# A graph-convolution layer on one core: A kept in DRAM as 8 KB runs, row blocks woven in pairs, and sparse products in 64-row pieces, up to eight at a time

## The chip, the cores and the metric

The kernel runs on one core of a Trainium2 chip. The metric is the device time of one execution in microseconds, as the median of several runs; less is better. Before the change three runs gave 1476.8, 1478.03 and 1470.32 us, a median of 1476.8 us.

## The reference

The inputs are `x` (8 x 4096 x 256, f32), `adj` (4096 x 4096, f32) and `W` (256 x 256, f32). `adj` is sparse: an entry is there with a probability that falls with its row and with its column, on the diagonal always, so the first rows and columns hold far more entries than the last.

```python
HW = jnp.einsum('bnf,fo->bno', H, W)              # H is x
A_norm = jax.nn.relu((A + A.T) * 0.5)
D = jnp.sum(A_norm, axis=1)
d_inv_sqrt = jnp.where(D > 0, D_safe ** (-0.5), 0.0)
DAD = d_inv_sqrt[:, None] * A_norm * d_inv_sqrt[None, :]
L_norm = jnp.eye(N, dtype=H.dtype) - DAD
out = jnp.einsum('nm,bmo->bno', L_norm, HW)
x = _layernorm(x + jax.nn.relu(out), axis=-1)
```

So the last product multiplies a sparse 4096 x 4096 matrix with a dense one of 4096 rows and 8 x 256 = 2048 columns (one row is 8 KB).

## The kernel before, in words

**Dense stage.** `adj` is cut into 8 x 8 blocks of 512 x 512. For each pair of blocks (i, j), (j, i) with i <= j, SP's DMA queue loads both (line 506; 1 MB each, in runs of 2 KB), TensorE transposes one in 128 x 128 tiles into a PSUM bank (line 516), VectorE adds the other (line 520), ScalarE applies relu with the factor 1/2 (line 524), and VectorE sums each row over groups of 32 columns (line 527). The sums give the degrees and, as flags, which rows of A have anything in which group of 32 columns. ScalarE's queue stores the block to `a_dram`, a 4096 x 4096 matrix laid out by rows, in runs of 2 KB (line 533). Beside this runs `form(m)`, which loads 128 rows of x (line 609, two loads of 512 KB in runs of 1 KB), transposes them (line 616), multiplies by W (line 627), scales by the rows' factor, and stores 128 rows of the product to `g_dram` (runs of 8 KB). `multiply` adds up the first output block, block 0, densely while this goes on (line 585). VectorE also builds the lists of the first units here (from line 250 on).

**List stage.** Blocks 1 to 31 of 128 output rows are left. They are handled in 16 units, unit u of blocks 2u+1 and 2u+2 (the last of block 31 alone), in the order of the table `SEQ`. A block is four groups of 32 columns, so a unit has eight groups. For each unit there is a list of the rows of A that have an entry in some of its groups. A tile of the list is 128 rows, as two halves of 64; a half belongs to one kind, a set of groups out of 15 such sets (`KINDS`, with `CAPS` and `FIRST` for their room and place). For each tile GpSimd issues two indirect DMAs, the rows of A cut to the groups in question (`ga`, line 1032) and the full rows of the product (`g`, line 1047, 128 rows of 8 KB, 1 MB), into one of 12 slots of a ring. There are 256 tiles. The slots are given back in the order in which they were filled, and each gather waits for a product named by `gather_ahead`, so that gathers keep pace with the products.

`steps_of(u)` cuts the unit's products into steps. A step fills the array once: one product of 128 rows by 128 columns, two of 128 x 64, four of 128 x 32, or pieces of 64 rows. Each step runs over the four PSUM banks of 512 columns that a block's 2048 columns take, and an f32 product runs as two passes of the array (two records in the profile). Two blocks of rows, the 256 first rows, are kept in SBUF for all units (`g_hub`), and are multiplied whole as 128 x 128 (with `gh`, the rows of A for them). When a block's last product is done, `finish` has ScalarE evict four banks (line 788) and VectorE add the residual x, take the statistics and normalise (lines 798, 807, 831); SP's queue stores the result (line 841, 1 MB in runs of 1 KB), and the residual of a later block is loaded by ScalarE's queue (line 782, likewise). The lists of units that come five, four, three and two places later are built by VectorE and TensorE between the products (`classify`, `lists`, `prepare`, `collect`).

If a unit's lists find no room, a flag sends the program into a dense loop at its end, which this input doesn't reach.

What sets the order: each engine's instructions are put by hand behind the last one of its engine (`queue`), so the order of the code is the order on the engine. On ScalarE's queue stand the stores of A and of the products, then the loads of residuals between evictions; on SP's the loads of `adj` and x, then the stores of the output; on GpSimd's the gathers.

## Time and profile before

| what | value |
|---|---|
| median of three runs | 1476.8 us |
| span of the profiled execution | 1496.2 us |
| TensorE matmul busy (PE) | 1420.1 us, 95% |
| VectorE (DVE) | 1025.2 us, 69% |
| GpSimd (POOL) | 745.6 us, 50% |
| ScalarE (ACT) | 368.7 us, 25% |
| moved by DMA | 540.52 MB, mean 361 GB/s |
| of it by GpSimd's indirect queue q0 / SP's q1 / ScalarE's q10 | 281.94 / 126.62 / 130.58 MB |

The profiled execution has a span of 1496.2 us, 19.4 us above the median of the timed runs. The dense stage lasts until about 565 us; the first list product stands at 587 us, the last ends at about 1484 us, and the rest of the span is the last block's end. PE's busy time includes modelled ends of matmuls. A DMA share of 1.00 stands for 16 DMA engines busy with packets all the time; it can come out a few per cent above 1 in a short stretch. In the profile "issue" is time in which an engine waited for nothing that the profile shows.

### The profile page before, as it was taken

How to read it: one execution, taken by the hardware profiler on the slowest of the kernel's cores; microseconds unless marked ns; L12 is line 12 of the kernel's file. 1: busy time of each engine (PE TensorE's matmuls, PEld its weight loads, DVE VectorE, ACT ScalarE, POOL GpSimd, SP SyncE). 2: the span in 40 equal slices, each digit the busy share in tenths (PEclk: the TensorE clock that was granted, in tenths of full speed). 3: DMA queues.
4: the chain of work that ended last, by engine and by line, in shares of the span. 5: the costliest groups of instructions: out<-in, count | busy, mean ns of one | idle time of the engine just before them, and what ended most of it. 6: DMA issues, size and time to landing. Idle time of an engine off the chain costs nothing.

```text
span 1496.2 us, 20479 instructions
## 1 busy us (share of the span) xinstructions
PE 1420.1 (95%) x6768; PEld 757.9 (51%) x6768; DVE 1025.2 (69%) x3010; ACT 368.7 (25%) x462; POOL 745.6 (50%) x1547
## 2 busy tenths in 40 slices
PE   7998988979999999999999999999999999998996
PEld 6777877766777764333333334333333333333342
DVE  4767558889596752356569678789898079797454
ACT  4555545434544460010100100100110011001102
POOL 2444010010322336756577677577677646666762
PEclk9999999989999999999999999999999999999998
DMA  9999999999999999979899899999999979988995
GB/s 340 360 377 381 406 346 337 393 385 338 379 356 341 371 392 373 373 270 379 332 377 379 338 402 407 366 388 403 398 382 377 387 259 341 354 316 321 402 404 220
DMA packets 215265, 540.52 MB, mean 361 GB/s; under 512 B 17751, under 2 KB 107527, under 8 KB 180839
## 3 DMA queue, kind: packets, MB, share of 16 engines
q0 software_dynamic: 53808, 281.94, 48.5%
q1 hardware_dynamic: 93200, 126.62, 24.4%
q10 hardware_dynamic: 68144, 130.58, 23.0%
q8 instruction: 56, 0.92, 0.2%
q14 instruction: 57, 0.46, 0.1%
HBM read 425.72 MB, written 136.34 MB: 376 GB/s over the span
## 4 chain that ended last, share of the span: by engine, by line
PE 62%; DMA 14%; DVE 11%; issue 7%; POOL 3%; ACT 3%; ACTq 0%; another core or an unknown queue 0%; DVEq 0%; POOLq 0%; SPq 0%
PE py L1263 45%; PE pg L627 8%; DMA a_dram<-sym 6%; DVE sym L520 4%; DMA g<-g_dram,gi 3%; PE xtr L616 3%; PE lead L585 3%; PE tr L516 3%; DMA xin<-in_x_dram 2%; POOL ga L1032 2%; ACT sym L524 1%; DVE sums L527 1%; POOL g L1047 1%; DMA g_dram<-held 1%; PE lists L450 1%
## 5 line engine op out<-in xcount | busy, mean ns | idle before, releaser
L1263 PE MATMUL py<-g,ga 128*32 128x512 f32 (+4 forms) x2880 | 644.8, 606 | 12.3 <-DMA g<-g_dram,gi 7.2
L1263 PEld LDWEIGHTS py<-g,ga 128*32 128x32 f32 (+4 forms) x2880 | 226.0, 138 | 402.0 <-issue 374.4
L1032 POOL DMA_INDIRECT ga<-a_dram,ai x256 | 277.6, 1084 | 181.3 <-issue 62.2
L1047 POOL DMA_INDIRECT g<-g_dram,gi x256 | 284.5, 1111 | 92.9 <-issue 77.6
L788 ACT ACTIVATE y<-py,minus_r 128x512 f32<-128x512 f32 x120 | 80.2, 686 | 796.3 <-PE py L1263 545.9
L627 PE MATMUL pg<-w_sb,xt 128*128 128x256 f32 x1024 | 233.4, 387 | 6.5 <-ACT xt L617 5.7
L1263 PE MATMUL py<-g_hub,gh 128*128 128x512 f32 x496 | 226.6, 601 | 0.5 <-DVE low L465 0.3
L627 PEld LDWEIGHTS pg<-w_sb,xt 128*128 128x128 f32 x1024 | 196.9, 195 | 34.5 <-ACT xt L617 6.6
L520 DVE TENSOR_TENSOR sym<-tr,adj 128x512 f32<-128x512 f32 x256 | 162.3, 684 | 59.0 <-PE tr L516 54.1
L527 DVE TENSOR_REDUCE sums<-sym 128x64 f32<-128x2048 f32 x64 | 145.7, 2282 | 69.5 <-ACT sym L524 69.5
L528 POOL TENSOR_SCALAR uses<-sums 128x64 uint8<-128x64 f32 x64 | 26.7, 417 | 271.1 <-DVE sums L527 236.9
L516 PE MATMUL tr<-ident,adj 128*128 128x128 f32 x1024 | 137.1, 281 | 20.5 <-DVE sym L520 14.3
L1263 PEld LDWEIGHTS py<-g_hub,gh 128*128 128x128 f32 x496 | 90.5, 190 | 123.6 <-issue 116.8
L524 ACT ACTIVATE sym<-sym 128x2048 f32<-128x2048 f32 x64 | 122.7, 1917 | 122.8 <-DVE sym L520 118.6
L516 PEld LDWEIGHTS tr<-ident,adj 128*128 128x128 f32 x1024 | 115.8, 143 | 50.9 <-DVE sym L520 31.1
L242 DVE TENSOR_TENSOR_SCAN incl_r<-carry,lists 128x32 f32<-128x32 bf16 x13 | 2.9, 221 | 182.0 <-PE lists L397 176.0
L429 DVE TENSOR_TENSOR hot<-iota_q,at 128x1024 bf16<-128x1024 f32 x64 | 74.5, 1220 | 34.0 <-PE lead L585 32.1
L798 DVE TENSOR_TENSOR xr<-xr,y 128x2048 f32<-128x2048 f32 x31 | 70.8, 2284 | 38.8 <-ACT y L788 32.1
L616 PE MATMUL xtr<-ident,xin 128*128 128x128 f32 x512 | 74.5, 299 | 17.9 <-DVE sym L520 9.0
L831 DVE TENSOR_SCALAR xr<-xr,mv,root 128x256 f32<-128x256 f32 x248 | 85.1, 416 | 1.1
L807 DVE BATCH_NORM_STATS2 stats<-xr 128x6 f32<-128x256 f32 x248 | 84.0, 413 | 1.1
L585 PE MATMUL lead<-gt,strip 128*128 128x512 f32 x176 | 82.4, 593 | 0.0
(164 smaller groups left out, 1040.1 us busy)
## 6 DMA issues: line engine op xcount, KB each, us to landing
adj<-in_adj_dram SPq DMA_DIRECT2D x64, 1024.0 KB
a_dram<-sym ACTq DMA_DIRECT2D x64, 1024.0 KB
out_dram<-xr SPq DMA_DIRECT2D x31, 1024.0 KB
xr<-in_x_dram ACTq DMA_DIRECT2D x28, 1024.0 KB
xin<-in_x_dram SPq DMA_DIRECT2D x44, 512.0 KB
g_dram<-gt ACTq DMA_DIRECT2D x22, 1024.0 KB
xin<-in_x_dram POOLq DMA_DIRECT2D x20, 512.0 KB
g_dram<-held ACTq DMA_DIRECT2D x10, 1024.0 KB
```

Source lines behind the costliest of these rows:

```text
L516: ins = nc.tensor.transpose(pt[:, c * P : (c + 1) * P], tji[:, c, a * P : (a + 1) * P], ident)
L520: nc.vector.tensor_add(sym[:, a, :], pt, tij[:, a, :])
L524: nc.scalar.activation(sym, sym, AF.Relu, scale=0.5)
L527: nc.vector.tensor_reduce(sums, sym.rearrange("p a (c q) -> p a c q", q=E), AX.X, ALU.add)
L585: nc.tensor.matmul(lead[c], lhsT=strip, rhs=g[:, c * S : (c + 1) * S], start=not done, stop=len(done) == NB - 1, skip_group_check=True,)
L616: nc.tensor.transpose(pt[:, k, c, :], xin[b // H][:, b % H + k, c * P : (c + 1) * P], ident)
L627: ins = nc.tensor.matmul(pg[:, k * FO : (k + 1) * FO], lhsT=xt[:, b + k, c, :], rhs=w_sb[:, c, :], start=(c == 0), stop=(c == FC - 1),)
L807: nc.vector.bn_stats(stats[:, b, :], z[:, b, :])
L831: nc.vector.tensor_scalar(z[:, b, :], z[:, b, :], mv[:, b, 0:1], rstd[:, b : b + 1], ALU.subtract, ALU.mult,)
L1032: rows = nc.gpsimd.indirect_dma_start(out=at if both else at[:, : E if one else P], out_offset=None, in_=a_pairs if both else a_groups if ...
L1047: nc.gpsimd.indirect_dma_start(out=gt, out_offset=None, in_=g_dram, in_offset=bass.IndirectOffsetOnAxis(ap=gi[:, t : t + 1], axis=0), boun ...
L1263: return nc.tensor.matmul(py[2 * u + 1 + b][c][cols, :], lhsT=at[ps, off + cols.start : off + cols.stop], rhs=gt[ps, c * S : (c + 1) * S], ...
```

## The change

**A in DRAM.** `a_dram` becomes 64 regions of 512 x 512, and in each region the four rows that one partition holds lie one after the other, so a partition stores 8 KB in one run. Everything that reads A (strips, diagonals, the kept rows, the gathers' indices) computes its places anew; the index of a row of a tile comes from a table of factors and offsets.

**Even and odd rows.** Of the 16 pairs of row blocks, all but the first and the last are woven: one block of a pair holds the even rows of the 256, the other the odd ones. A partition then holds two neighbouring rows, so residual loads and output stores of a pair run over 2 KB, and are issued as two halves of 1 MB. `adj` is loaded as two DMAs of 512 KB in place of one of 1 MB; the transposes take every second column as their stationary operand, and the adds read every second column of the other block. A block of `adj` that lies half in a woven pair and half in one that isn't needs two adds of 256 columns per row group instead of one of 512. The loads of x in `form` stay in runs of 1 KB.

**Units.** Unit u holds blocks 2u and 2u+1, unit 0 holds blocks 1 and 30, and unit 15 holds block 31. A table `UNITS` names for each unit the place and room of eight single groups, of sets of any groups (a mask, a room, a place), and of the full set, with an order of its tiles. The constants for this are one table loaded by DMA; before, GpSimd wrote them with 752 small memsets.

**Products.** Every gathered tile is multiplied in pieces of 64 rows by 32 columns, up to eight at a time (two halves by four groups of columns). Both halves of the array work on different banks; where a half comes to a bank that the other half had, a `nop` on TensorE waits for the products of two turns before. Only the kept blocks are multiplied as 128 x 128.

**Slots.** A ring slot is given back as soon as its last product is issued, in any order (`free`), and gathers no longer wait for a product to keep pace. Two kept tiles of 16 KB in each partition, used in turn by the units, hold the residuals. One more unit's lists are begun in the dense stage (five).

By the schedule there are 234 steps before (144 of one full 128 x 128 product, 51 of two pieces, 33 of four, 2 of six, 4 of eight) and 212 after (62 full, 150 tiled: 87 of eight pieces, 30 of seven, 15 of six, 18 of one to five). Both fetch 256 tiles. Counted from the input, the lists name 29952 rows before and 30258 after.

```diff
-        a_dram[i * S : (i + 1) * S, j * S : (j + 1) * S].rearrange("(a p) s -> p a s", p=P), sym
+    def region(i, j):
+        return a_dram[(i * NS + j) * S : (i * NS + j + 1) * S, :].rearrange("(p a) s -> p a s", a=A)
...
+            nc.scalar.dma_start(region(i, j), sym)
...
+    def pair_of(ap, w, bs):
+        return ap[bs, w * T * P : (w + 1) * T * P, :].rearrange("b (p t) f -> p b t f", t=T)
...
+            for w in range(A // T):
+                lo = i * S + w * T * P
+                order = "(p t) s -> p t s" if woven(lo // (T * P)) else "(t p) s -> p t s"
+                nc.sync.dma_start(
+                    t[:, w * T : (w + 1) * T], adj[lo : lo + T * P, j * S : (j + 1) * S].rearrange(order, t=T)
+                )
...
+            near = [t for t in turns if todo[t]][:reach]
+            cells = sorted((op for t in near for op in todo[t]), key=lambda op: turn[op[0]] + lag * op[2])
+            step = [
+                op for h in range(2) for j in range(QU) for op in [op for op in cells if op[1:4:2] == (h, j)][:1]
+            ]
...
+            while free and asked < len(order):
+                gather(*order[asked], free.pop(0))
+                asked += 1
...
+            for n in range(NC):
+                for k, op in enumerate(step):
+                    c = (n + (flip ^ op[1]) * NC // 2) % NC if tiled else n
+                    if tiled and n >= NC // 2 and k == 0:
+                        with queue("pe"):
+                            turn = nc.tensor.nop()
+                        tc.add_manual_dep(turn.ins, turns[n - NC // 2].ins.name, mybir.DependencyInfo(...))
+                    ins = product(u, op, c, opens[op], last[op])
+                turns.append(ins)
```

On TensorE, early in the first unit of the list stage, before: `py_b_c` is bank c of the unit's block b, `g` and `ga` are a tile's rows, and 64x512 means that a product has 64 output rows (columns of A) and 512 columns. The end of a kept block's step, a step of one full product and half a step of two pieces:

```order
L1263 MATMUL py_0_2_5871<-g_hub_5723,gh_0_5786 128x512
L1263 MATMUL py_0_3_5872<-g_hub_5723,gh_0_5786 128x512
L1263 MATMUL py_0_0_5869<-g_5743,ga_5776 128x512
L1263 MATMUL py_0_1_5870<-g_5743,ga_5776 128x512
L1263 MATMUL py_0_2_5871<-g_5743,ga_5776 128x512
L1263 MATMUL py_0_3_5872<-g_5743,ga_5776 128x512
L1263 MATMUL py_0_0_5869<-g_5747,ga_5777 64x512
L1263 MATMUL py_0_0_5869<-g_5751,ga_5778 64x512
```

The same place after the change, the end of the second kept block's step and half of the first tiled step (four of its pieces to a bank are shown for banks 0 and 2):

```order
L1357 MATMUL py_1_2_5296<-g_hub_5096,gh_0_5161 128x512
L1357 MATMUL py_1_3_5297<-g_hub_5096,gh_0_5161 128x512
L1357 MATMUL py_0_0_5242<-g_5104,ga_5149 32x512
L1357 MATMUL py_0_0_5242<-g_5108,ga_5150 32x512
L1357 MATMUL py_1_0_5294<-g_5108,ga_5150 32x512
L1357 MATMUL py_0_0_5242<-g_5108,ga_5150 32x512
L1357 MATMUL py_0_2_5244<-g_5104,ga_5149 32x512
L1357 MATMUL py_0_2_5244<-g_5108,ga_5150 32x512
L1357 MATMUL py_1_2_5296<-g_5108,ga_5150 32x512
L1357 MATMUL py_0_2_5244<-g_5108,ga_5150 32x512
```

Where a full product gave one instruction to a bank, eight pieces now stand, four on the bank of one half and four on the bank of the other.

On SP's queue at the start of the program, where `xin` is x and `adj` a block of the matrix, before:

```order
L609 DMA xin_1_183<-in_x_dram 128x4x256
L506 DMA adj_0_236<-in_adj_dram 128x4x512
L506 DMA adj_1_325<-in_adj_dram 128x4x512
L506 DMA adj_0_327<-in_adj_dram 128x4x512
L609 DMA xin_0_379<-in_x_dram 128x4x256
```

And after:

```order
L774 DMA xin_1_170<-in_x_dram 128x4x256
L667 DMA adj_0_223<-in_adj_dram 128x2x512 x2
L667 DMA adj_1_265<-in_adj_dram 128x2x512 x2
L667 DMA adj_0_268<-in_adj_dram 128x2x512 x2
L774 DMA xin_0_325<-in_x_dram 128x4x256
```

The order is the same; each load of `adj` is now two. On ScalarE's queue the residual loads of a unit stay where they were, between the evictions of two blocks, but are one pair in halves (`res`, 128x4x512 twice) where two blocks (`xr`, 128x8x256 each) stood.

More of the change, by code (lines that the diff above doesn't have):

```diff
@@ L142, with owner @@
+    halves = [halves_of(u) for u in range(NU)]
+    tiles = [len(h) for h in halves]
+    def owner(u, t):
+        top, bottom = halves[u][t]
+        if top & (top - 1) == 0 and bottom & (bottom - 1) == 0:
+            return ALONE
+        m = top | bottom
+        return 2 if m & 15 and m >> QU else int(m >> QU > 0)
     tmax = max(tiles)
@@ L951, in steps_of @@
-        held = range(HUBS[u])
-        out = [full(-1, 0)] if HUBS[u] else []
-        starts = [full(t, 0) for t in whole[15]]
-        if not out and starts:
-            out.append(starts.pop(0))
-        if blocks(u) == 1:
-            return out + [full(-1 - h, 0) for h in held[1:]] + starts + rounds + [full(t, 0) for t in whole[0]]
-        out += weave(rounds[:first_b1], [full(-1 - h, 0) for h in held[1:]], starts)
-        out += [full(-1, 1)] if HUBS[u] else []
-        rows = [[full(t, 0), full(t, 1)] for t in whole[0]]
@@ L961, in steps_of @@
-        between = [[r] for r in rounds[first_b1 : max(last_b0 + 1, first_b1)]]
-        out += chain.from_iterable(weave(between, rows))
-        out += weave(
-            [full(-1 - h, 1) for h in held[1:]],
-            [full(t, 1) for t in whole[240]],
-            rounds[max(last_b0 + 1, first_b1) :],
-        )
-        last = max(q for q, step in enumerate(out) if any(op[2] == 0 for op in step))
-        begin = next(q for q, step in enumerate(out) if any(op[2] for op in step))
-        only = [q for q in range(begin + 1, last) if all(op[2] for op in out[q])]
@@ L974 @@
+        return [step for q in range(n + 1) for step in at[q] + rounds[q : q + 1]]
     with (
+        tc.tile_pool(name="res_0", bufs=1) as res_0,
+        tc.tile_pool(name="res_1", bufs=1) as res_1,
         tc.tile_pool(name="ypool", bufs=2) as ypool,
@@ new lines @@
+            last = {op: not any(left[cell] for cell in cells) for op, cells in cells_of.items()}
+            tiled = step[0][1] is not None
+            turns = []
+            for n in range(NC):
[4 more added lines that the diff above has]
+                            turn = nc.tensor.nop()
+                        tc.add_manual_dep(
+                            turn.ins,
+                            turns[n - NC // 2].ins.name,
+                            mybir.DependencyInfo(mybir.DependencyClass.Sync, mybir.DependencyReason.DATA),
+                            reason="the halves of the array change banks",
+                        )
+                    ins = product(u, op, c, opens[op], last[op])
+                turns.append(ins)
@@ L1325 @@
+            flip ^= tiled
+            for t in dict.fromkeys(op[0] for op in step):
+                uses_left[u, t] -= sum(op[0] == t for op in step)
+                if t >= 0 and not uses_left[u, t]:
+                    free.append(slot_of[u, t])
+            gather_ahead()
             run_later(2)
```

1086 lines of the change are left out of this document (591 added, 495 removed), and 32 rows, old and new, of tables (CAPS, FIRST).

## The prediction

> **What bounds the kernel now.** I read the page's chain first, then a table of the busy time of each engine by stretches of the span, then the DMA queues of the stretches.
>
> ```profile
> PE 62%; DMA 14%; DVE 11%; issue 7%; POOL 3%; ACT 3%; ACTq 0%; another core or an unknown queue 0%; DVEq 0%; POOLq 0%; SPq 0%
> PE py L1263 45%; PE pg L627 8%; DMA a_dram<-sym 6%; DVE sym L520 4%; DMA g<-g_dram,gi 3%; PE xtr L616 3%; PE lead L585 3%; PE tr L516 3%; DMA xin<-in_x_dram 2%; POOL ga L1032 2%; ACT sym L524 1%; DVE sums L527 1%; POOL g L1047 1%; DMA g_dram<-held 1%; PE lists L450 1%
> ```
>
> The chain names TensorE, above all the list products of line 1263. The table shows what else is full there; its columns are the stretch, its length, the busy us of PE, PEld, DVE, ACT and POOL, the granted clock, the DMA share and GB/s.
>
> ```profile
> 50.00:150.00 100.00, 92.66 (x550) 76.26 (x549) 73.09 (x98) 54.09 (x65) 44.68 (x582) 0.98 1.04 376
> 150.00:250.00 100.00, 90.41 (x490) 74.51 (x488) 63.10 (x98) 49.44 (x59) 9.79 (x23) 0.93 0.98 362
> 250.00:350.00 100.00, 91.26 (x505) 73.43 (x504) 85.00 (x179) 48.01 (x53) 9.55 (x22) 0.95 1.03 382
> 350.00:450.00 100.00, 93.96 (x536) 73.21 (x535) 80.96 (x199) 48.59 (x59) 23.61 (x41) 1.00 0.97 359
> 450.00:565.00 115.00, 110.09 (x548) 80.91 (x547) 74.70 (x149) 55.08 (x63) 36.66 (x63) 0.97 0.98 369
> 587.00:700.00 113.00, 111.66 (x471) 41.41 (x471) 67.20 (x237) 5.99 (x10) 75.04 (x72) 1.00 0.89 335
> 700.00:900.00 200.00, 195.43 (x906) 73.70 (x903) 133.25 (x482) 18.58 (x28) 139.47 (x133) 1.00 0.97 368
> 900.00:1150.00 250.00, 247.15 (x1117) 94.54 (x1116) 216.39 (x781) 24.28 (x36) 173.95 (x165) 1.00 1.01 388
> 1150.00:1300.00 150.00, 147.76 (x629) 55.74 (x627) 88.31 (x316) 12.73 (x19) 90.27 (x89) 1.00 0.92 342
> 1300.00:1484.00 184.00, 176.05 (x761) 68.62 (x758) 113.86 (x406) 21.69 (x33) 109.48 (x106) 0.98 0.92 347
> ```
>
> So there are two bounds side by side. The dense stage (to 565 us) keeps the DMA engines at 0.97 to 1.04, with PE at 90 to 96%. The list stage (587 to 1484 us, 897 us) has PE at 96 to 99%, but the DMA share is 0.89 to 1.01 too: 113 x 0.89 + 200 x 0.97 + 250 x 1.01 + 150 x 0.92 + 184 x 0.92 = 854 us of DMA work in 897. Whatever is taken from PE there can give at most the distance down to that second wall, and what is taken from the DMA engines moves the wall.
>
> The span is 1496.2 us, the median of the timed runs 1476.8, so the profiled execution is 19 us dearer. I make the sum in differences and apply it to the median; where the 19 us may come from matters below.
>
> **Part 1: fewer, fuller steps of the list products.** A step is one pass over the array for all four banks. I cut the next table at the first instruction of a step and of the following one: a full 128x128 step, a step of four 128x32 pieces, one of six 64x32 pieces, then five that hold eight or six such pieces.
>
> ```profile
> 587.23:590.76 3.53, 3.53 (x12) 1.34 (x15) 1.00 1.02 421
> 590.76:594.33 3.57, 3.57 (x33) 0.94 (x30) 1.00 0.85 329
> 777.99:781.57 3.58, 3.58 (x49) 1.01 (x44) 1.00 1.00 411
> 640.60:646.57 5.97, 5.97 (x68) 1.73 (x68) 1.00 0.91 309
> 707.24:718.67 11.43, 8.78 (x65) 2.03 (x62) 1.00 0.99 393
> 833.34:839.81 6.47, 5.92 (x49) 1.32 (x45) 1.00 1.06 409
> 1290.77:1300.61 9.84, 8.34 (x65) 1.98 (x61) 0.90 0.94 329
> 1342.40:1354.25 11.85, 8.30 (x65) 1.97 (x61) 0.71 0.96 329
> ```
>
> A full step takes 3.53 us, a tiled one 3.57 however many pieces it holds. Before there are 234 steps, after 212 (62 full ones for the kept blocks, 150 tiled), by the schedule. PE's need was 144 x 3.53 + 90 x 3.57 = 830 us and becomes 62 x 3.53 + 150 x 3.57 = 754: **-76 us of PE work**. What is left of the 897 us after these 830 and the 28 us of the next paragraph, 39 us, is list building and short waits, so PE alone would need 754 + 39 = 793.
>
> The price is the instruction stream: a step of eight issues 64 products and 64 weight loads where a full one issues 8 and 8; 132 steps of six to eight pieces stand there, against six before. The last five rows say that such a step does not always run in 3.57 us. The chain through the one at 707 shows why.
>
> ```profile
> 709.32 0.82 issue
> 710.14 0.63 PE py L1263 x2
> 710.76 0.09 issue
> 710.86 0.59 PE py L1263
> 711.44 0.82 issue
> 712.26 1.01 PE py L1263 x3
> 713.28 0.41 issue
> ```
>
> PE waits there for nothing that the profile shows: instructions come too slowly. The excess over 3.57 is 2.4, 7.9, 2.9, 6.3 and 8.3 us in those five (the last also waits for gathered rows) and 0 in the third row: 28 us over six steps, a mean of 4.6. Bounds of the added cost: nothing (the row at 777.99) to 132 x 4.6 = +607 us. Which end? Three things speak for nothing in a timed run. The 28 us are close to the 19 us that the profiled execution is longer than the timed median. The step that begins at 707.24 runs for 2.1 us before the first such wait, at 709.32. And short matmuls elsewhere are issued faster still: 32 products with 32 weight loads in 0.80 us (25 ns each pair, where a step of eight needs 56).
>
> ```profile
> 383.50:384.30 0.80, 0.80 (x32) 0.80 (x31) 1.00 1.05 405
> ```
>
> I take it that recording the instructions is what holds them up, and use 3.57. I also take 0 for the 300 waits by which the two halves of the array change banks: between a wait and the products it waits for lies a whole turn of 3.57 / 4 = 0.89 us, so they have ended; at the outside 0.1 us each, 30 us of PE time, which part 2's wall hides.
>
> **Part 2: longer DMA runs.** The queues, in three stretches (the first 100 us, 556 to 570, 900 to 1150): packets, MB, share of 16 engines.
>
> ```profile
> q10 hardware_dynamic: 6153, 11.81, 30.6%
> ...
> q10 hardware_dynamic: 866, 5.30, 92.3%
> ...
> q0 software_dynamic: 13861, 76.42, 76.7%
> q10 hardware_dynamic: 10367, 10.45, 12.5%
> q1 hardware_dynamic: 9742, 9.81, 11.1%
> ```
>
> 2 KB runs (stores of A): 0.306 x 1600 us / 6153 = 80 ns, 24.1 GB/s on an engine. 8 KB runs (stores of products, mean packet 6.1 KB): 0.923 x 224 / 866 = 239 ns, 25.6 GB/s. 1 KB runs: x reads 0.125 x 4000 / 10367 = 48 ns, output writes 0.111 x 4000 / 9742 = 46 ns. So:
> - A's 64 MB of stores: 67.1 MB / 16 x (1/24.1 - 1/25.6 per GB/s) = 174 us - 164 = **-10 us** of DMA time in the dense stage.
> - x loads and output stores of 28 of 32 blocks, from 1 KB to 2 KB at some 85 ns per 2 KB: (28672 x 48 - 14336 x 85 + 28672 x 46 - 14336 x 85) / 16 = 16 us; less in practice since the last stores overlap nothing; **-14 us** in the list stage.
> - The new list pieces name 306 more rows of 8 KB (29952 to 30258, counted from the input): 2.5 MB / (16 x 25 GB/s) = **+6 us** there.
>
> The list stage's DMA work becomes 854 - 14 + 6 = 846 us. From 900 to 1150 the share held 1.01 with PE full as well, so the wall stands at 846 / 1.01 = 838, and with the start and the last unit's tail, where nothing is left to fetch, I take 848. PE's 793 lies under it: the stage changes from PE-bound with DMA close to DMA-bound, PE idling about 50 us on arriving rows. Against what? The timed stage before is 897 less the 19 us that the profile adds: 878. **848 - 878 = -30 us.** Freeing ring slots in any order only helps to stay near that wall.
>
> **Part 3: the dense stage.** Its loads of adj are split into halves (128 DMAs for 64), in runs of 2 KB as before; transposes and adds read every second column.
>
> ```profile
> L520 DVE TENSOR_TENSOR sym<-tr,adj 128x512 f32<-128x512 f32 x256 | 162.3, 684 | 59.0 <-PE tr L516 54.1
> L387 DVE TENSOR_REDUCE slot<-pos_k x16: 921/928/958, 272.1 to 1330.4; 128x32 f32<-128x448 f32 x16
> L246 DVE TENSOR_TENSOR pos_k<-incl_k,lists x12: 621/622/622, 652.0 to 1306.7; 128x448 f32<-128x448 f32 x12
> L225 POOL MEMSET group_of<- 64x1 bf16 x304 | 29.1, 96 | 10.9
> ```
>
> Cost of a strided add: nothing, to the ratio of a widely strided reduce to a contiguous add over 448 elements, 928/622: 256 x 684 x 0.49 = +86 us of DVE. A step of two elements is nearer to contiguous than that reduce's 32, so I take nothing. Of the 256 adds 64 are split in two, at some 0.16 us of overhead +10 us, and lists for one more unit are prepared here, +20 us. DVE has 376 us busy from 50 to 565, at most 85 of 100, so it can take these 30 us beside the DMA. POOL loses its small memsets, off the chain. The 10 us of DMA time end on the path only where DMA is last; PE and DVE waits share the chain here, so I take **-6 us** (0 to -13).
>
> The Trainium skill, "DMA: Bandwidth & Descriptors", section Bandwidth, "Measured", speaks against the split: it wants transfers of 1 MiB or more, and its fit has 2.0 us fixed in each DMA; an estimate from that page is 64 x 2.0 = +128 us if nothing overlapped. The trace has 512 KB loads of x among those of adj and a share of 1.04 from 50 to 150 us, so I count nothing and keep 2% for it.
>
> **Sum.** 1476.8 - 30 - 6 = 1441; the likeliest case spans 1407 (wall at 846/1.03 = 821, dense stage -13) to 1462.
>
> **The rivals.**
> - *DMA hides the whole PE gain* (17%): shorter PE time makes gathers overlap more densely, and each takes longer. For it: 0.97 to 1.01 between 700 and 1150 already. Only part of the -18 us of DMA remains: 1462 to 1480.
> - *PE keeps its gain* (9%): the share reaches 1.04 as in the dense stage and the DMA wall falls under PE: 793 - 878 - 13 gives about 1380, to 1407.
> - *Steps of eight are short of instructions without a profile too* (17%). Slower: 132 x 4.6 = 607 us makes PE's need about 1400, so 1476.8 - 878 + 1400 = about 2000. It decides from (878 - 793) / 132 = 0.64 us of excess in a step. Against it is the 19 us difference; for it, that no row says why the queue ran dry. In a sentence apart: the Trainium skill, "Runtime: NRT & Kernel Launch", section on the preamble and postamble, puts a profile's total about 6.2 us above the reported time; if all of that lay in the span, only 13 of the 28 us would be the recording's, and half the excess would be real, about 1700. No run here shows that gap alone.
> - *DVE becomes the dense stage's bound* (5%): +86 and +30 on 376 in 515 us fills the stretch from 250 to 350 (85 of 100) past its end: 1475 to 1500.
> - The split loads cost as above (2%): dearer than 1500.
>
> **How the numbers follow.** Forecast 50%: 1441. This kernel's measurement can tell about 0.5%, 1469 to 1484. Faster: 50 + 9 + half of the first rival, 9 = 68%. Same: 8 + 2 = 10%. Slower: 17 + 3 + 2 = 22%. The range leaves out the instruction shortage and the split: 1385 to 1485.
>
> **What would show it.** In the profile after: DMA share 0.98 or more through the list stage and PE idle for gathered rows by tens of us (part 2); stores of A near 310 ns a packet; steps of eight at 3.57 us in the timed run, seen as a timed median far below the span, which the recording would stretch by hundreds of us. A median that stretches with the span, PE's "issue" ending most of its idle time, proves me wrong; so does a list stage of 793 or less, or DVE above 95% before 565 us.

## The result, and the profile after

The changed kernel takes **1455.84 us** (median of 4 runs, 1454.27 to 1463.11) against 1474.69 (1470.32 to 1478.03) for the kernel before on the same chip: a ratio of **0.9888 [0.9854, 0.9922]**. The two medians lie 18.9 us apart; by the interval of the ratio the gain is between 11.5 and 21.5 us. The forecast was 1441, 36 us less. The direction was right, the time lies in the range, and the gain is about half of what was forecast (18.9 of 36 us by the medians, 1.1 of 2.4% by the ratio). The profiled execution of the changed kernel has a span of 1452.6 us and a time of its own of 1454.47.

That first profile of the kernel before was an execution of 1496.2 us. A second one (run `before_again`, on a chip called B below: span 1469.2, time 1470.92) is nearer to the median and serves as the base from here on. The stages by the first and the last list product:

| us | first profile of before | `before_again` | after |
|---|---|---|---|
| first row sum of the dense stage | 22.9 | 21.7 | 26.7 |
| first list product | 587.1 | 581.3 | 595.0 |
| last list product | 1483.2 | 1455.1 | 1438.1 |
| list stage (last less first) | 896.1 | 873.7 | 843.1 |
| span | 1496.2 | 1469.2 | 1452.6 |

So the list stage gains 30.6 us, where -30 was forecast; a third profile of the kernel before, but for split loads (`before_split`, below), has 873.9 for it as well. The dense stage, for which -6 was forecast, loses. How much it loses is better read from the medians than from single executions, since the first list product of the kernel before stands anywhere from 571.2 (`before_split`) to 587.1: 30.6 - 18.9 = **+11.7 us**, and 9 to 19 by the interval of the ratio.

The chain of the changed kernel, by engine and then by line:

```profile
PE 45%; DMA 28%; DVE 14%; issue 7%; POOL 4%; ACT 2%; SPq 0%; POOLq 0%; DVEq 0%; ACTq 0%
PE py L1357 23%; DMA g<-g_dram,gi 19%; PE pg L792 10%; PE tr L681 5%; DMA ga<-a_dram,ai 4%; PE xtr L781 3%; DVE sym L690 3%; PE lead L750 3%; DVE sums L697 2%; DMA res<-in_x_dram 2%; POOL ga L1109 2%; POOL g L1116 2%; DMA a_dram<-sym 2%; DMA adj<-in_adj_dram 2%; ACT sym L694 1%
```

List products held 45 and 46% of the chain in the first profile of before and in `before_again`, and hold 23% now; arriving rows of `g` rose from 3 and 5% to 19%, and VectorE from 11 and 9% to 14%. The two halves of the program show up in it: DMA now shares the list stage with the products, and VectorE has taken some of the dense stage.

### The profile page after: what moved, and what is told of

Its sections match the earlier page's. It is cut to its first block, busy times and chain, and to the rows that moved or that the text cites. A ratio compares the mean times of both kernels' runs of the same rounds, so it can differ in the third digit from the quotient of the medians.

```text
span 1452.6 us, 30775 instructions
## 1 busy us (share of the span) xinstructions
PE 1356.2 (93%) x12288; PEld 740.6 (51%) x12288; DVE 1058.3 (73%) x2861; ACT 360.6 (25%) x462; POOL 708.9 (49%) x759
## 3 DMA queue, kind: packets, MB, share of 16 engines
q10 hardware_dynamic: 31416, 132.20, 22.9%
## 4 chain that ended last, share of the span: by engine, by line
PE 45%; DMA 28%; DVE 14%; issue 7%; POOL 4%; ACT 2%; SPq 0%; POOLq 0%; DVEq 0%; ACTq 0%
PE py L1357 23%; DMA g<-g_dram,gi 19%; PE pg L792 10%; PE tr L681 5%; DMA ga<-a_dram,ai 4%; PE xtr L781 3%; DVE sym L690 3%; PE lead L750 3%; DVE sums L697 2%; DMA res<-in_x_dram 2%; POOL ga L1109 2%; POOL g L1116 2%; DMA a_dram<-sym 2%; DMA adj<-in_adj_dram 2%; ACT sym L694 1%
## 5 line engine op out<-in xcount | busy, mean ns | idle before, releaser
L1357 PE MATMUL py<-g,ga 64*32 64x512 f32 x8368 | 567.0, 602 | 22.3 <-DMA g<-g_dram,gi 22.2
L1357 PEld LDWEIGHTS py<-g,ga 64*32 64x32 f32 x8368 | 191.3, 108 | 353.8 <-issue 261.9
L1109 POOL DMA_INDIRECT ga<-a_dram,ai x256 | 287.6, 1124 | 82.5 <-issue 59.8
L1357 PE MATMUL py<-g_hub,gh 128*128 128x512 f32 x496 | 229.2, 606 | 12.5 <-DVE row L628 12.4
L690 DVE TENSOR_TENSOR sym<-tr,adj 128x512 f32<-128x512 f32 (+1 forms) x320 | 166.4, 575 | 25.1 <-PE tr L681 22.9
L681 PE MATMUL tr<-ident,adj 128*128 128x128 f32 x1024 | 145.0, 291 | 14.0 <-DVE sym L690 10.7
L681 PEld LDWEIGHTS tr<-ident,adj 128*128 128x128 f32 x1024 | 136.5, 200 | 38.5 <-issue 16.1
L578 DVE TENSOR_TENSOR hot<-iota_q,at 128x1024 bf16<-128x1024 bf16 x64 | 74.4, 1215 | 32.1 <-PE lead L750 32.1
L960 DVE TENSOR_TENSOR res<-res,y 128x2048 f32<-128x2048 f32 x31 | 70.9, 2287 | 35.9 <-ACT y L950 35.6
L969 DVE BATCH_NORM_STATS2 stats<-res 128x6 f32<-128x256 f32 x256 | 86.9, 411 | 0.7
L993 DVE TENSOR_SCALAR res<-res,mv,root 128x256 f32<-128x256 f32 x248 | 83.6, 409 | 1.1
## 6 DMA issues: line engine op xcount, KB each, us to landing
g_dram<-held ACTq DMA_DIRECT2D x10, 1024.0 KB, 11.5
```

Source lines behind the costliest of these rows:

```text
L681: ins = nc.tensor.transpose(pt[:, c * P : (c + 1) * P], tji[:, c, columns(i, a)], ident)
L690: nc.vector.tensor_add(out_, new, old)
L969: nc.vector.bn_stats(stats[:, b, :], z[:, b, :])
L993: nc.vector.tensor_scalar(z[:, b, :], z[:, b, :], mv[:, b, 0:1], rstd[:, b : b + 1], ALU.subtract, ALU.mult,)
L1109: nc.gpsimd.indirect_dma_start(out=to, out_offset=None, in_=view, in_offset=bass.IndirectOffsetOnAxis(ap=ai[:, t : t + 1], axis=0),)
L1357: return nc.tensor.matmul(py[BLOCKS[u][b]][c][cols, :], lhsT=at[rows, off + cols.start : off + cols.stop], rhs=gt[rows, c * S : (c + 1) * ...
```

## Where the time went in the fast executions

**The list stage.** Busy time of each engine over the whole stage, before (`before_again`) and after; the columns are those of the prediction's table (PE, PEld, DVE, ACT, POOL, granted clock, DMA share, GB/s).

```profile
581.30:1455.10 873.80, 862.13 (x3875) 331.26 (x3873) 616.83 (x2217) 84.87 (x125) 590.85 (x560) 1.00 0.97 370
```

```profile
595.00:1438.10 843.10, 808.32 (x9385) 301.04 (x9383) 621.95 (x2026) 74.98 (x122) 594.03 (x545) 0.98 1.00 391
```

PE's busy time falls by 53.8 us and its idle time rises from 11.7 to 34.8 us, by 23.1; the difference is the 30.7 us. The DMA share rises from 0.97 to 1.00 of a shorter stage. PE is still busy for 96% of it, so this row alone does not say which of the two bounds it. The groups of list products show how large the gain of PE is, before and then after (busy us, mean ns of one record):

```profile
L1263 PE MATMUL py<-g,ga 128*32 128x512 f32 (+4 forms) x2880 | 630.4, 602 | 6.5 <-DMA g<-g_dram,gi 6.5
...
L1263 PE MATMUL py<-g_hub,gh 128*128 128x512 f32 x496 | 225.8, 600 | 0.0
```

```profile
L1357 PE MATMUL py<-g,ga 64*32 64x512 f32 x8368 | 567.0, 602 | 22.3 <-DMA g<-g_dram,gi 22.2
...
L1357 PE MATMUL py<-g_hub,gh 128*128 128x512 f32 x496 | 229.2, 606 | 12.5 <-DVE row L628 12.4
```

That is 856.2 us against 796.2, 60 us less where 76 were forecast (830 less 754): 567.0 / 150 gives 3.78 us for a tiled step, not 3.57. Six steps in a row, early in the stage, take 3.62 each:

```profile
602.01:623.70 21.69, 21.69 (x385) 7.72 (x385) 16.32 (x53) 0.00 (x0) 17.43 (x17) 1.00 0.99 369
```

Not one of the six stalls: eight pieces a bank are issued in time on this chip. The idle time that grew is the 22.2 us for rows of `g` in the group above, and the 12.4 us for `row`, an index that VectorE makes.

**The dense stage.** From 50 to 565 us, before (`before_again`) and after, and for the changed kernel the two stretches in which VectorE builds the lists of the first units:

```profile
50.00:565.00 515.00, 478.65 (x2628) 375.46 (x2627) 376.00 (x719) 254.79 (x297) 127.70 (x735) 0.98 1.01 374
```

```profile
50.00:565.00 515.00, 478.53 (x2631) 391.99 (x2630) 406.06 (x749) 254.48 (x299) 94.28 (x176) 0.97 0.97 362
...
250.00:350.00 100.00, 83.35 (x453) 68.25 (x452) 92.81 (x184) 44.08 (x49) 11.19 (x21) 0.91 0.91 339
350.00:450.00 100.00, 96.86 (x550) 78.00 (x550) 89.57 (x171) 49.42 (x60) 21.54 (x35) 1.00 0.98 363
```

VectorE has 30.1 us more to do, close to the +30 of the prediction. But they are not spread over the 515 us: they make VectorE 93% busy from 250 to 350, and there the DMA share falls to 0.91 and PE to 83%. A mean of 79% over the stage hid a stretch in which the engine was all but full.

TensorE has more to do as well. From the start to the first list product, before (`before_again`) and after, and then the transposes of `adj` and their weight loads (PEld) in both, where the second number is the mean ns of one:

```profile
0.00:581.30 581.30, 536.33 (x2894) 418.00 (x2895) 401.70 (x768) 280.74 (x329) 153.60 (x981) 0.98 1.00 372
0.00:595.00 595.00, 547.27 (x2905) 439.53 (x2906) 430.18 (x809) 279.15 (x329) 108.83 (x209) 0.97 0.97 360
```

```profile
L516 PE MATMUL tr<-ident,adj 128*128 128x128 f32 x1024 | 137.3, 281 | 21.0 <-DVE sym L520 15.6
L516 PEld LDWEIGHTS tr<-ident,adj 128*128 128x128 f32 x1024 | 115.3, 143 | 52.0 <-DVE sym L520 33.5
```

```profile
L681 PE MATMUL tr<-ident,adj 128*128 128x128 f32 x1024 | 145.0, 291 | 14.0 <-DVE sym L690 10.7
L681 PEld LDWEIGHTS tr<-ident,adj 128*128 128x128 f32 x1024 | 136.5, 200 | 38.5 <-issue 16.1
```

Between these two executions the stage is 13.7 us longer. PE's busy time makes 10.9 of that and its idle time 2.7. The transposes take 7.7 us more: their stationary operand is now every second column, and loading it takes 200 ns where it took 143. No run takes this cost away alone, so what it is worth on the path isn't shown. VectorE's added time over the whole stage is 28.5 us, of it 4.4 for the adds (162.0 to 166.4 us) and some 24 for the rest, above all the lists.

## The experiments

These runs fell on four chips, called B, C, D and E here; the record doesn't name the chip of the first result (A), which may be B. The kernel before took 1472.2 us on B and 1490 to 1496 on C, D and E, which is little. The changed kernel took 1456 on A and 1672 to 1681 on C and D: 12 to 13% slower than the kernel before. Runs on C, D and E are therefore compared only with runs beside them, and tell about the dense stage as before, since the first list product stands within 6 us of chip A's there.

**The kernel before once more, and with its loads of `adj` split (chip B).**

> The kernel before, once more, unedited. The recording theory of the prediction (the stalls of 8-piece steps come from the recording): a profile again has them, a span of about 1496 us, some 20 us above the timed median of 1475. Rival (chance of one execution: the stalls or other delays came in that execution alone): a span of 1468 to 1477, 2 us below its own time, and the five steps with 8 and 6 pieces run in about 3.6 us each.

> The kernel before with each 1 MB load of adj as two loads of 512 KB, nothing else. If the split costs the dense stage its time: 3 to 8 us slower than the kernel before (1478 to 1483 for 1475), the first reduce of line 527 at about 26 us where it was at 23. If the split is free: within 2 us of 1475 and the first reduce at 23.

```diff
-            nc.sync.dma_start(t, adj[i * S : (i + 1) * S, ...].rearrange("(a p) s -> p a s", p=P))
+            for w in range(2):
+                lo = i * S + w * 2 * P
+                nc.sync.dma_start(t[:, 2 * w : 2 * w + 2], adj[lo : lo + 2 * P, ...].rearrange(...))
```

`before_again` took 1470.92 us with a span of 1469.2. Its five steps of eight and six pieces, recorded as in the first profile, where they took 5.97, 11.43, 6.47, 9.84 and 11.85 us:

```profile
634.76:638.35 3.59, 3.59 (x69) 1.10 (x72) 1.00 0.99 345
698.24:701.83 3.59, 3.59 (x66) 1.10 (x65) 1.00 0.99 371
762.03:765.61 3.58, 3.58 (x49) 1.01 (x49) 1.00 1.00 390
1271.83:1275.88 4.05, 4.05 (x65) 1.35 (x65) 1.00 0.91 329
1317.12:1327.76 10.64, 7.37 (x66) 2.07 (x65) 0.84 0.94 301
```

Four of the five have lost their stalls or nearly so; the last waits for gathered rows, as it did before. So 20 of the 28 us in the first profile did not come from recording. Were they chance, or the chip? The first profile's span of 1496.2 us lies above every timed execution of the kernel before on A and B (1466.8 to 1478.2) and among those on C, D and E (1482.9 to 1507.1). The kept traces hold a second sign: how long after the end of a TensorE product the semaphore update comes that reports it. By the semaphore records of the list stage 90 of 423 updates come more than 0.4 us later in the first profile, 1 of 498 in `before_again`, 1 of 725 in the changed kernel on A and 241 of 706 on C. So the first profile looks like one of a chip of the kind of C, though the record doesn't name its chip. The 878 us that the prediction put for a timed list stage were near the 873.7 measured, but for another reason than the one it gave. The split takes 1467.87, 0.9986 [0.9969, 1.0002]: it costs nothing that can be seen.

**The table of constants loaded after the start; its effect and that of counting later (chip B).**

> The changed kernel with the table of constants loaded after the first eight copies on ScalarE rather than at its start. If the table's load is what makes the start 3.7 us later: the first reduce at about 23 us where it was 26.7, and the whole 3 us shorter, 1453 for 1456. If the split loads do it: the first reduce stays at 26 to 27 and the time at 1456.

> The changed kernel with the count products of each unit's lists in the dense stage put one piece of the schedule later (both matchings). Theory of the wait (PE stands 13 us at 305 us for VectorE's scan, with transposes queued behind): that wait falls under 4 us, the dense stage ends 5 to 9 us earlier, 1447 to 1451. Theory of the load (VectorE, 24 of 25 us busy between 300 and 375, is itself the bound): PE's wait only changes its place, 1454 to 1458.

```diff
-    for h in range(2):
-        nc.scalar.dma_start(tables[h * L : (h + 1) * L], table[h : h + 1].to_broadcast([L, ends[-1]]))
...
+        with tc.issue_after(last_act):
+            for h in range(2):
+                nc.scalar.dma_start(tables[h * L : (h + 1) * L], table[h : h + 1].to_broadcast(...))
```

```diff
-        whole = [patterns, count_place, more, more, count_place_more, more, count_place_rest]
+        whole = [patterns, skip, count_place, more, more, skip, count_place_more, more, count_place_rest]
```

`after_table`: the first row sum comes at 22.4 us instead of 26.7, the first list product at 591.2 instead of 595.0; 1452.71 us, 0.9871 [0.9845, 0.9896]. Two loads of 284 KB that stood ahead of x and `adj` thus make the start some 4 us later (the profiles of the changed kernel without this edit have the first row sum at 25 to 27 us); that the first list product gains as much is one execution against one. It is the lowest time of the study, but its interval overlaps the changed kernel's, so it isn't shown to be faster than that.

`after_count` moves one wait: in the changed kernel TensorE stands 13 us in the dense stage for VectorE's `ahead_of`, since the count is queued right behind it.

```profile
318.53 0.59 PE L454 MATMUL q<-ahead_of,ones 128*128 128x495 bf16 x1 [13.12 <-DVE ahead_of L404]
```

I took this wait for the loss. With the count two parts later it is gone, and the kernel is slower than without the edit, and slower than either expectation: 1470.01, 0.9977 [0.9958, 0.9996], first list product at 604.9. From 300 to 325 us, the changed kernel and then `after_count`:

```profile
300.00:325.00 25.00, 10.49 (x60) 8.96 (x59) 24.07 (x48) 5.75 (x3) 5.80 (x12) 0.73 0.84 317
```

```profile
300.00:325.00 25.00, 13.11 (x69) 10.48 (x68) 24.41 (x55) 6.32 (x4) 6.05 (x12) 0.75 0.96 354
```

VectorE is full in both (24 of 25 us), and PE waits about half the time in both, now for `sym` instead of `ahead_of`. A new wait comes later, since a buffer of `adj` that the lists borrow is held two parts longer:

```profile
381.63 0.67 PE L681 MATMUL tr<-ident,adj 128*128 128x128 f32 x2 [8.73 <-DMA adj<-in_adj_dram]
```

So taking this wait away gains nothing: it is where the loss can be seen. Whether the 8.7 us of the new wait hide a small gain, the run doesn't show.

**VectorE's work, early and late, and A in runs of 2 KB again (chip C).**

> The changed kernel with the row sums taken twice for parts 4 to 23 of the dense stage (about 50 to 180 us, no lists built there): 20 x 2.28 = 46 us more of VectorE. VectorE has 73 to 78 of 100 us busy there, so if it is not the bound: the 28th part comes 5 to 20 us later and the whole is 5 to 20 us slower.

> The same 46 us of VectorE in parts 28 to 47, about 210 to 400 us, where the lists are built. Theory of the load (VectorE is the bound there): 35 to 46 us slower, about 1491 to 1502, twice the early dose or more. Theory of the wait (only PE's single wait of 13 us costs): 5 to 20 us, like the early dose.

> The changed kernel with the four rows of a partition stored 128 rows apart inside each region of A, so the stores run over 2 KB again; indices follow. If DMA time ends on the dense stage's path: about 10 us slower than the changed kernel (1466 for 1456), all of it before the first list product (595 to 605). If VectorE and PE set the dense stage: 0 to 4 us slower, the first list product at 595 to 599, stores of A at 80 ns per 2 KB instead of 310 per 8 KB.

```diff
             nc.vector.tensor_reduce(sums, sym.rearrange("p a (c q) -> p a c q", q=E), AX.X, ALU.add)
+            if 4 <= len(flags) < 24:
+                nc.vector.tensor_reduce(sums, sym.rearrange("p a (c q) -> p a c q", q=E), AX.X, ALU.add)
```

```diff
-        return a_dram[(i * NS + j) * S : (i * NS + j + 1) * S, :].rearrange("(p a) s -> p a s", a=A)
+        return a_dram[(i * NS + j) * S : (i * NS + j + 1) * S, :].rearrange("(a p) s -> p a s", p=P)
```

The row sums of 20 parts are taken twice, 45.6 us of VectorE, in parts 4 to 23 or, for `dve_late`, 28 to 47. The runs take 1716.38 and 1735.33 us. The first list product moves from 594.5 (the changed kernel on that chip, `after_again`) to 612.2 and to 622.6: +18 us where few lists are built, +28 where they are, that is 0.39 and 0.61 us for each us of VectorE. For the late dose 35 to 46 us were expected if VectorE is the bound there and 5 to 20 if not; 28 lies between. So VectorE is partly the bound all along the stage, and most where the lists are. At these rates the change's 30 us cost 12 to 18 us. With the table's 4 and up to 8 for the transposes, less what the stores gain, the sum is above the 11.7 measured (9 to 19), so the terms overlap, and how the loss divides among them isn't shown. One difference speaks for a share of the transposes: the late dose of VectorE shows mostly as idle PE (21 of its 28 us up to the first list product), where the change made PE itself busier (10.9 of 13.7).

`after_2k` (1702.8 us in all) puts the first list product at 600.5. Five executions with the changed stores on the same chip have it at 593.3 to 598.4, and those on D and E at 592.5 to 600.2. So the gain of the 8 KB runs is 2 to 7 us, one execution against five, and may be less. That they are cheaper for the DMA engines is plain; ScalarE's queue from the start to the first list product, `after_2k` and then `after_again` (packets, MB, share):

```profile
q10 hardware_dynamic: 38872, 101.52, 43.0%
q10 hardware_dynamic: 14296, 101.52, 41.6%
```

0.430 x 600.5 - 0.416 x 594.5 = 10.9 us of DMA time, where 10 were forecast, on engines whose share in this stage is down to 0.97.

**Lists spread over more parts (chip D).**

> The changed kernel with the table of constants loaded after ScalarE's first eight copies, and with the lists of the second to fifth unit begun 2 to 3 parts later in the dense stage (1, 10, 18, 25, 31 for 1, 8, 15, 22, 28). The table gave 4 us at the start. If VectorE's list work crowded together is what costs: the first list product at 583 to 588 where the changed kernel has it at 594 to 595 and the one with the table alone at 591. If only its sum counts: 590 to 592.

```diff
-            for u, at in (first, 1), (second_, 8), (third, 15), (fourth, 22), (fifth, 28):
+            for u, at in (first, 1), (second_, 10), (third, 18), (fourth, 25), (fifth, 31):
```

With the late table as well. First list product at 586.9, beside 592.5 for the changed kernel on the chip (`after_c`): -5.6 us, of which the table has 4. Spreading alone gives 2 us at most, one execution against one, and none of it is seen in the whole: 1671.59 us against 1672.05.

**Residuals and outputs in runs of 1 KB (three chips).**

> The changed kernel with the residual loads and output stores of the list stage block by block in runs of 1 KB, rows still woven. If DMA is the list stage's bound after the change: 12 to 17 us slower, the list products spread over 856 to 862 us where it was 844, DMA share still 1.00. If PE is the bound: 0 to 4 us slower.

> The changed kernel with residual loads and output stores in runs of 1 KB, again. Where steps of eight run at 3.6 us: if DMA is the list stage's bound, 12 to 17 us slower than the changed kernel beside it; if PE is, 0 to 4. Where they run short of instructions: 0 to 4, since PE then sets the pace.

> The changed kernel with residual loads and output stores in runs of 1 KB. Where steps of eight take 3.6 us: 12 to 17 us slower than the changed kernel if DMA bounds the list stage, 0 to 4 if PE does. Where they are short of instructions: 0 to 10.

> The changed kernel with residual loads and output stores in runs of 1 KB. On a chip where steps of eight take 3.6 us: ratio to the kernel before 0.997 to 1.000 (12 to 17 us above the changed kernel's 0.989) if DMA bounds the list stage, 0.989 to 0.992 if PE does. On a chip that is short of instructions: 1.125 to 1.135, as twice before.

```diff
-                bs = slice(n * H, (n + 1) * H)
-                engine.dma_start(tile_of...[:, bs], pair_of(x, u, bs))
+                m = BLOCKS[u][n]
+                engine.dma_start(xr[m], rows_of(x, m))
```

This was to show whether the DMA engines bound the list stage: 14 us more of DMA work should lengthen it by as much, or by nothing. All four runs fell on C, D and E: 1706.54 and 1690.34 (C), 1683.52 (D) and 1714.04 us (E, where the changed kernel itself wasn't run). Beside the changed kernel there, 1690.34 against 1680.73 (C) and 1683.52 against 1672.05 (D), +10 and +11 us; the list stage is 6 and 16 us longer. But the intervals overlap (on C 1.1247 to 1.1385 and 1.1207 to 1.1336), list stages that no edit touched differ as much on C (1072.5, 1087.0 and 1087.8 us in `after_again`, `dve_early` and `dve_late`), and the stage is bound otherwise there. So the question stays open, and on chips like A it wasn't tried. The price of a packet is shown; the output stores of the changed kernel on A, from 900 to 1150 us:

```profile
q1 hardware_dynamic: 4619, 9.19, 9.8%
```

0.098 x 4000 / 4619 = 85 ns for 2 KB, as the prediction took.

**The changed kernel on the other chips, and half of its DMA, products or pieces.**

> The changed kernel once more, unedited, to stand on the same chip as the next three. If this chip issues TensorE's instructions as the one of the first result: 1453 to 1460 us, list products spread over 843 to 847 us, steps of eight pieces 3.6 us. If it issues them as the one of the last four runs (kernel before at 1496, the changed one's variants at 1703 to 1735): about 1690 to 1700, list products over 1085 to 1100 us.

> The changed kernel, unedited, beside the next three. 1453 to 1460 where a step of eight pieces takes 3.6 us, 1675 to 1695 where it is short of instructions.

> The changed kernel that gathers the rows of the product for every second tile only (after each slot has been filled once) and multiplies what the slot still holds; everything else stays. DMA work of the list stage falls by about 120 MB, 300 us, so what is left is PE's own need. If PE's need is the 793 us of the prediction: list products over 790 to 800 us where they took 843. If PE's need is nearer to the wall, because of turnovers and lists: 810 to 830. Where instructions are short: no shorter than beside it.

> The changed kernel with the pieces of 64 x 32 multiplied for two of the four banks of each block only (each half of the array keeps two banks, and the waits between halves go); kept blocks whole, all gathers stay. PE's need falls by some 270 us. If DMA is the wall at a share of 1.00: list products over 835 to 845 us, as before this edit. If PE was the bound: well below 830. Where instructions are short: also about 840, since half of them are gone.

> The changed kernel without the pieces of the lower 64 rows of each tile (steps that hold only such pieces issue one of them): at most four pieces of 64 x 32 in a step, half the instructions in the same 3.6 us, all gathers, steps, banks and waits as they were. Theory of the instruction rate: no shortage on any chip, list products over 840 to 860 us, 1450 to 1470 in all, even where the changed kernel takes 1672 to 1681. Theory of the waits between halves: still short there, above 1600.

```diff
+            if k in filled and asked % 2:
+                slot_of[u, t] = k
+                got[u, t] = (at, gt, who)
+                return
```

```diff
-            for n in range(NC):
+            for n in range(NC // 2 if tiled else NC):
```

```diff
-                for k, op in enumerate(step):
+                for k, op in enumerate([op for op in step if not tiled or not op[1]] or step[:1]):
```

In this order: `half_dma` gathers the rows of `g` for every second tile only, `half_pe` makes two of four turns of a tiled step and so has no wait between the halves, `half_rows` multiplies the pieces of one half of the array only and keeps the waits. They take 1558.9 and 1513.26 (C) and 1736.45 us (E). `after_again` takes 1680.73 on C, 1.1272 [1.1207, 1.1336], `after_c` 1672.05 on D, 1.1208 [1.1163, 1.1252]. Two stretches of 64 products on C, a step of eight each, and then the waits of PE in the list stage there (us, times, longest):

```profile
660.25:665.09 4.84, 3.79 (x64) 1.15 (x64) 0.00 (x0) 0.00 (x0) 2.92 (x4) 1.00 0.93 306
665.13:670.48 5.35, 4.84 (x64) 1.68 (x64) 0.00 (x0) 0.00 (x0) 3.23 (x4) 1.00 0.95 392
```

```profile
PE py L1357 <- remote: 122.6, 47, 9.1
PE py L1357 <- PE py L1357: 26.3, 37, 1.5
```

"remote" is an event that the view finds on no queue. The records of the waiting instructions name the semaphore: in all of these waits it is that of TensorE's own products (in one of them another beside it), as where a half takes over a bank of the other, and in none that of a gather. On A the 22.2 us that PE waited stood on gathers' semaphores. The list stages of the four, with the columns as above, in the order `after_again`, `half_dma`, `half_pe` (all on C) and `half_rows` (on E), each from its own profile:

```profile
594.50:1666.90 1072.40, 905.67 (x9381) 298.35 (x9383) 622.23 (x2026) 77.14 (x122) 566.02 (x545) 0.91 0.83 307
```

```profile
595.00:1542.50 947.50, 842.10 (x9383) 288.56 (x9383) 620.45 (x2026) 75.78 (x123) 447.83 (x422) 0.96 0.65 224
```

```profile
593.30:1496.60 903.30, 746.87 (x5200) 241.25 (x5199) 617.74 (x2026) 78.81 (x123) 591.28 (x546) 0.84 0.96 364
```

```profile
593.80:1726.20 1132.40, 993.92 (x5209) 292.23 (x5207) 619.67 (x2026) 82.41 (x123) 573.16 (x545) 0.77 0.78 291
```

The stage is 229 us longer on C than on A: 132 of it PE idle (166.7 against 34.8), 97 more of PE busy, at a clock of 0.91 instead of 0.98. Neither the DMA (share 0.83) nor VectorE (622 us, as on A) bounds it. Half the instructions and the same waits (`half_rows`) do not help: 1132 us, and "remote" waits of 119.7 us remain. Without the waits between the halves (`half_pe`) these shrink to 7.6:

```profile
PE py L1357 <- DVE row L628: 48.9, 10, 8.1
PE py L1357 <- issue: 29.1, 56, 2.4
...
PE py L1357 <- remote: 7.6, 2, 3.8
```

So on these chips it is the waits between the halves that are paid, not the number of instructions, save for 29 us of "issue". The waits do not make the reports late: without them (`half_pe`) 162 of 420 updates still come more than 0.4 us after the product's end. Whether the update is late, or the product itself ends later than its modelled end, the trace can't tell. With less DMA traffic (`half_dma`) the excess halves, where no change was expected on such a chip, and why, I can't say. `half_pe` says something else besides: with half the products the stage still takes 903 us (about 840 were expected) at a DMA share of 0.96, so 867 us of DMA work. That is near the 846 of the prediction, and PE's own work can't be the reason there, though PE's waits for `row` (48.9 us) may have a part in it.

**Wider pieces where neighbours agree (chip D).**

> The changed kernel with pieces of one step that stand side by side in one tile, one half and one block joined into 64 x 64 or 64 x 128 (1046 pieces become 903; steps, banks and waits stay). Theory of the instructions: where steps are short of them, the list products take 40 to 90 us less than beside it (1072 before), by steps of eight at 5.24 us, of seven at 4.6 and of six at 3.9; where they are not, no change (within 3 us). Theory of the waits between halves: no change anywhere.

```diff
+            pieces = {op[1:4:2]: op for op in step}
+            joined = []
...
+                        if op and j % c == 0 and all(o and o[0] == op[0] and o[2] == op[2] for o in row):
...
+                        joined.append((op[0], h, op[2], j, w))
-            rounds.append(step)
+            rounds.append(joined)
```

Pieces of the same rows for the same block are joined to 64 or 128 columns, which leaves 8241 PE records of 9385. It was to help if instructions were short, and to change nothing if the waits were the cause; neither came. It takes 1951.56 us, 1.3041 [1.2987, 1.3095], 280 us more than `after_c`. Pieces of different widths in one turn don't run side by side but one width after the other; the stretch of a piece of 64 columns, before the pieces of 32 in the same turn begin, once at full and once at half clock:

```profile
618.73:619.73 1.00, 1.00 (x4) 0.19 (x6) 0.83 (x6) 0.00 (x0) 0.70 (x2) 1.00 1.02 258
655.32:657.21 1.89, 1.89 (x5) 0.28 (x6) 0.00 (x0) 0.00 (x0) 0.00 (x0) 0.50 0.00 0
```

Where all pieces have one width, a turn takes 0.89 us; here each width takes about as long on its own. Fewer, unequal pieces are dearer than eight equal ones.

## Why the prediction was right or wrong, point by point

- **What bounds the kernel: right, as far as it is shown.** The list stage went from PE-bound with DMA close to DMA share 1.00, as Part 2 says, and lasts 843.1 us where 848 was taken. `half_pe`, with 867 us of DMA work and half of PE's products, fits it on chip C. That an added us of DMA work lengthens the stage isn't shown on any chip.
- **Part 1: right in sign, too large.** "-76 us of PE work" became -60: the 754 of after came out at 796, since the mean tiled step takes 3.78 us and not 3.57, and the 830 of before at 856. PE was busy for 808 us, so its idle time was 35 us and not the forecast 50. The second wall hid the error.
- **"I take it that recording the instructions is what holds them up": the reason fell, the value held on A.** `before_again` was recorded too, and 20 of the 28 us were gone. The stalls go with the chip, by all that the traces show: the first profile has the marks of C, where a tiled step of the changed kernel takes 1.5 us more on average (229 / 150). That the result fell on a chip like A was luck: on C and D the same kernel took 1672 to 1681 us, far outside the range.
- **"I also take 0 for the 300 waits": right on A, wrong on C, D and E.** There the outside bound of 0.1 us each, 30 us, was too low: the two rows of PE's waits on C, 122.6 and 26.3 us, make 0.5 us for each of the 300. A turn of 0.89 us between a wait and its product was enough only where a product's end is reported at once.
- **Part 2's price of runs: right.** The 8 KB runs saved 10.9 us of DMA time where 10 were taken, and a packet of 2 KB took 85 ns as taken. That the 14 us shorten the list stage by as much isn't shown.
- **Part 3 failed: "I take -6 us (0 to -13)".** It is +11.7 (9 to 19). The size of VectorE's added work was right (28.5 to 30.1 us for 30). The sentence that it "can take these 30 us beside the DMA" is the step that failed: 376 of 515 us was a mean, the lists go where VectorE was at 80 to 85 of 100 already, and each us of VectorE that the doses added cost 0.39 to 0.61 us. A second step failed beside it: the transposes that read "every second column" are named and put at nothing without a reason, and took 7.7 us more of PE, in a stage where PE is busy for 92% of the time. A third term was missing: the table of constants ahead of the first loads, 4 us. The gain that was to outweigh such terms came as DMA time, and 2 to 7 us of it may have reached the path. How the loss divides among the three stays open. The strided adds cost nothing, as taken (a median of 679 ns against 680), and the split loads too.
- **The sum.** By the medians 17 us of the forecast's 36 are missing. Part 3 is 17.7 of them (11.7 + 6); the list stage gave 0.6 more than its -30.
- **The rivals.** VectorE as the bound of the dense stage, 5% and worked out as +86 and +30 us, was the nearer to what happened, with the +30 alone and most in one place. The instruction shortage did not happen on A; on the other chips long steps came, at a third of the price (1.5 us, not 4.6), and for the most part with another cause.
- **The signs.** DMA share 1.00 and 22.2 us of PE idle for gathered rows came as named. So did one of the signs of being wrong, VectorE above 95% before 565 us: 24.07 of the 25 us from 300 to 325.

## What to carry to other kernels

Read the slack of an engine from the stretch where the added work will stand, not from the stage: by the mean of 73% there was room for 30 us of VectorE, and yet an added us cost 0.4 to 0.6. When a layout changes, price every operand that is read with a step, the weights of a transpose too. When a long wait ends on an engine that is full, moving the wait moves it elsewhere. And take the profile of the kernel before more than once and on more than one chip before a rival is judged by it; a gain that rests on taking it that waits "have ended" in time may be a loss on the next chip.

## What the runs showed of the hardware

- The same two kernels compare as 0.989 on one chip and 1.12 to 1.13 on others, while the kernel before differs by 1.5% between them. On A a wait for a product of PE's own was released about 0.1 us after that product's end, 0.6 us before it was needed; on C the weight load that waits started mostly 0.4 to 1.2 us after PE had run dry, sometimes 2 to 9.1. Why is open: from 600 to 1440 us 8 KB packets take 349 ns on average there against 326, but 317 on both in the dense stage, and instruction fetches are alike (57 and 72 packets of that queue from 600 to 1400).
- In the list stages on C and E PE is granted a lower clock than on A, as their rows show (0.77 to 0.96 against 0.98). It doesn't go with these waits alone: `half_pe`, with 7.6 us of them, has 0.84. One and the same full step takes 6.04 us at 0.60 and 3.63 at 1.00 (`half_rows`, kept blocks):

```profile
645.32:651.36 6.04, 6.04 (x12) 2.38 (x16) 0.00 (x0) 0.00 (x0) 4.56 (x5) 0.60 0.54 170
731.15:734.78 3.63, 3.63 (x12) 1.44 (x16) 3.36 (x21) 0.00 (x0) 2.92 (x3) 1.00 0.86 275
```

- Pieces of different widths in one turn cost about a turn for each width (above), which no row of before had shown.
- A weight load of 128 x 128 f32 whose columns stand two elements apart took 209 ns in the median, a contiguous one 140 (the transposes of `adj`, 1024 in each profile, on A and C against B).
- Every execution's time was its span and 1.7 to 2.4 us (1454.47 and 1452.6; 1470.92 and 1469.2), so the spans can be compared with medians nearly as they stand.
